# The attention products of a gated cross-attention kernel on TensorE: two 64x128 tiles in place of four 64x64 tiles

## The chip, the cores and the metric

The kernel runs on one core of one Trainium2 chip. The metric is the device time of one execution in microseconds (us), the median of several runs. A profile is one further execution, whose span (first to last instruction) is a little shorter than its time.

## The reference

Inputs in float32: `x` is 8 x 1024 x 1024, `ctx_1024` (the memory) 8 x 64 x 512, `W_mem` 1024 x 512, `W_gate` 1024 x 2048, a bias and a norm weight of 1024 each.

```python
memory_proj = jnp.einsum('bme,de->bmd', memory, W_mem)
scores = jnp.einsum('bnd,bmd->bnm', hidden_states, memory_proj) / jnp.sqrt(jnp.float32(D))
attn = jax.nn.softmax(scores, axis=-1)
memory_context = jnp.einsum('bnm,bmd->bnd', attn, memory_proj)
gate_input = jnp.concatenate([hidden_states, memory_context], axis=-1)
gate = jax.nn.sigmoid(jnp.einsum('bnf,df->bnd', gate_input, W_gate) + b_gate)
fused = hidden_states + gate * memory_context
return _rmsnorm(fused, norm_w)
```

A memory has only 64 rows, so the contraction of `attn` with anything of the memory is 64 long, half of TensorE's 128 rows.

## The kernel before

The 8192 tokens are worked in 16 query tiles (`q`) of 512 tokens, two to each of the 8 memories. The setup, up to about 80 us, computes `mp`, the projected memory, and `mg`, which is `mp` times the second half of `W_gate` plus the bias. Both are kept side by side in one tile, `mg`: partitions 0 to 63 hold `mp` of the present memory (for the context), partitions 64 to 127 hold `mp` times the gate weight (for the memory's part of the gate). `attnT` holds the softmaxed scores turned so that the 64 memory rows lie on partitions, once on 0 to 63 and once, with some sums and differences, on 64 to 127.

The large product, `x` times the first half of `W_gate`, is done for each query tile by a two-level Strassen scheme. `outer_product` (L949) handles one of seven outer products, in the order 1, 6, 7, 5, 4, 2, 3 (`ORDER`, L648); each is itself seven inner products of a 128-token block by 256 columns, issued by `product` (L961) as two 128x128 by 128x256 matmuls. The inner products go to the PSUM banks `af`, `ed` (two sets that alternate), `b` (tile `kB`) and `c` (tile `kC`). VectorE, ScalarE and GpSimd take the sums between them.

The attention enters in *visits* (`visit`, L853). A visit stands for one block of 128 tokens and one half of 512 columns, and issues two kinds of product. The first gives the context of these tokens, from partitions 0 to 63 of `attnT` and `mg` into a bank `pc`. The second adds the memory's part of the gate from partitions 64 to 127, into the bank `af` or `ed` in which the Strassen products of the same rows are summed. In one case of each four (`second and r == 0`) this second product is cut into two of 256 columns. Visits stand in blocks of four, between the inner products `kC` and `ed` of outer product 4 (visits of 5 and 4) and of outer product 3 (visits of 2 and 3). In the last query tile the second block is cut into two blocks of two visits. Before the change each product is issued twice, once for tokens 0 to 63 and once for tokens 64 to 127 (`TOKENS`, L849): as its stationary operand is 64 rows by 64 columns it takes one quarter of TensorE, and the quarter follows from the partitions of the operands and of the output. The four quarters are: upper rows or lower rows (context or gate part), left columns or right columns (first or last 64 tokens).

`scores` (L400) computes the next query tile's scores, in tiles `psT`, also in 64x64 quarters: two row halves by two column halves at each of eight steps of the depth, 32 matmuls. From the first query tile on, each `scores` of a next tile stands right behind the visits of outer product 3 in TensorE's order; the first tile's own stands alone among the inner products.

The order on each engine is the order in which the code issues (`pin`, L90); `at` and `mid` (L641, L644) put the side work at numbered slots. `mm` (L92) issues every matmul, so L93 is the line of all of them in the profile, and L96 that of all two-operand sums. A float32 matmul appears in the trace as two passes, each with its own weight load (LDWEIGHTS) and MATMUL record. In a row such as `64*64 64x512` the first pair is the rows and columns of the stationary operand, the second the moving operand.

Of the kernel before, what the change touches and what calls it, by code (L numbers as in the profile page):

```python
# [15 lines left out]
P = 128  # L16
# [4 lines left out]
def tile_gated_cross_attention_rmsnorm(  # L21
# [44 lines left out]
    M, E = mem.shape[1:]  # L66
# [25 lines left out]
    def mm(o, lhsT, rhs, start, stop):  # L92
        pin(nc.tensor.matmul(o, lhsT, rhs, start=start, stop=stop, skip_group_check=True))  # L93
# [7 lines left out]
    def t4k(pool, shape, tag, name):  # L101
        return pool.tile(shape, F32, tag=tag, name=name)
# [31 lines left out]
    for k in range(KD):  # L134
        t = t4k(*((gpool, [P, D], "gate") if k < 7 else (apool, [P, D], "s4")), f"w2_{k}")
# [363 lines left out]
    def upper(left):  # L499
        return left ^ 2 if left < 4 else left  # L500
# [345 lines left out]
    EXT = {5: (1, 1, 2), 4: (1, 0, 2), 2: (0, 0, 0), 3: (0, 1, 4)}  # L846
    SECOND = {4: 5, 3: 2}
    NEG = {4: 6, 3: 7}
    TOKENS = slice(0, P // 2), slice(P // 2, P)  # L849
    sets = 0  # L850
    held = {}

    def visit(q, o, r, pc, k, k1=None):  # L853

        row, h, g = EXT[o]
        at_, mg = attnTs[q], mgs[q // QPB]
        second = o in SECOND
        cols = slice(h * H, (h + 1) * H)
        for t in TOKENS:
            mm(pc[t, :], at_[0:M, 2 * row + r, t], mg[0:M, cols], True, True)  # L860
        if second and r == 0:
            for n, left in ((0, g + r), (1, NEG[o])):
                part = mg[M:P, h * H + n * C : h * H + (n + 1) * C]
                apart = n == 1 and k1 is not None
                for t in TOKENS:
                    dst = k1[t] if apart else k[t, n]
                    mm(dst, at_[M:P, upper(left), t], part, apart, True)
        else:
            whole = k.rearrange("p n c -> p (n c)")
            for t in TOKENS:  # L870
                mm(whole[t, :], at_[M:P, upper(g + r), t], mg[M:P, cols], second, True)

    def pre(q, o, u3, u4):

# [74 lines left out]
    def outer_product(q, o):  # L949
# [31 lines left out]
        if second:  # L981
            if alone:
                pcs = [bank(t, [P, H], f"pc{q}_{o}_{r}") for r, t in enumerate("bc")]
            else:
                f = SECOND[o]
                faf, fed, fu3, fu4 = held.pop((q, f))
                frow, fh, _ = EXT[f]
                fp = [bank(t, [P, H], f"pc{q}_{f}_{r}") for r, t in enumerate("bc")]
                pcs = [ps_ctx.tile([P, H], F32, tag="ctx", name=f"pc{q}_{o}_{r}") for r in range(2)]
                visit(q, f, 0, fp[0], faf)  # L990
                visit(q, f, 1, fp[1], fed)
            if alone:
                apart = ps_ctx.tile([P, C], F32, tag="ctx", name="apart")
                visit(q, o, 0, pcs[0], af, apart)
            else:
                visit(q, o, 0, pcs[0], af)
            visit(q, o, 1, pcs[1], ed)
# [121 lines left out]
```

## Time and profile before

| | |
|---|---|
| median of 3 runs | 945.98 us (945.97 to 946.01) |
| profiled execution: its time, its span | 945.9 us, 944.1 us |
| TensorE matmul (PE) busy | 933.0 us, 99% of the span |
| weight loads (PEld) busy, beside PE | 726.3 us, 77% |
| VectorE (DVE) busy | 798.4 us, 85% |
| GpSimd (POOL) busy | 736.7 us, 78% |
| ScalarE (ACT) busy | 420.3 us |
| MATMUL records | 5560 |

PE's busy time covers overlapping records, since several tiles work at once and a record also holds the way through the array; how much time a stage takes is read from the starts of the records. A query tile takes 53.35 us in the steady part (the visits' first block starts at 217.37, 270.72 and 324.07 us).

### The profile page before, as it was taken

What the parts mean: (1) busy time and instruction counts of PE and PEld (TensorE: products, weight loads), DVE (VectorE), ACT (ScalarE), POOL (GpSimd) and SP (SyncE); (2) the same over time, 40 slices, a digit from 0 to 9 for tenths busy, and PEclk for the clock granted to TensorE, in tenths of its full rate; (3) what the DMA queues carried; (4) which work ended last, traced back from release to release, by engine and by line L of the source; (5) the groups of instructions that cost most, each with busy time, mean ns of one, the idle gap of its engine ahead of it and who ended that gap; (6) DMA issues with size and microseconds to landing.
All of it is one profiled execution on the core that took longest, in us unless ns stands there. A gap on an engine that the chain in (4) does not pass through costs nothing.

```text
span 944.1 us, 15840 instructions
## 1 busy us (share of the span) xinstructions
PE 933.0 (99%) x5560; PEld 726.3 (77%) x5560; DVE 798.4 (85%) x1273; ACT 420.3 (45%) x1089; POOL 736.7 (78%) x815
## 2 busy tenths in 40 slices
PE   9999999999999999999999999999999999999995
PEld 8546778787877778787877778687877778787774
DVE  6989888888887888888887888888887888888887
ACT  3001437263644527263643627263543617264556
POOL 5998968788586868778596868778696868868695
PEclk9999999999999999999999999999999999999998
DMA  9956664482919365491919366391918456391632
GB/s 377 287 149 157 112 124 111 113 179 48 209 45 182 99 137 131 103 187 41 216 46 175 93 143 137 90 201 32 220 51 168 102 134 146 80 205 33 134 153 90
DMA packets 70928, 128.44 MB, mean 136 GB/s; under 512 B 12352, under 2 KB 49216, under 8 KB 70592
## 3 DMA queue, kind: packets, MB, share of 16 engines
q1 hardware_dynamic: 61664, 93.86, 37.8%
q0 software_dynamic: 9184, 33.56, 19.5%
q8 instruction: 45, 0.74, 0.3%
q14 instruction: 35, 0.29, 0.1%
HBM read 87.56 MB, written 41.68 MB: 137 GB/s over the span
## 4 chain that ended last, share of the span: by engine, by line
PE 94%; DVE 3%; POOL 1%; issue 1%; ACT 1%; POOLq 0%; DVEq 0%; ACTq 0%
PE af L93 31%; PE ed L93 20%; PE pc L93 10%; PE kC L93 10%; PE kB L93 10%; PE pg L93 5%; PE psT_af L93 5%; PE pm L93 3%; POOL gate L96 1%; DVE gate L96 1%; DVE u L96 0%; PE psT_ed L93 0%; PE pz L93 0%; PE psT_b L93 0%; POOL l L96 0%
## 5 line engine op out<-in xcount | busy, mean ns | idle before, releaser
L96 POOL TENSOR_TENSOR gate<-gate,u 128x512 f32<-128x512 f32 (+1 forms) x224 | 243.5, 1099 | 153.7 <-DVE u L96 152.8
L717 ACT ACTIVATE gate<-gate 128x512 f32<-128x512 f32 x127 | 79.9, 630 | 181.5 <-DVE gate L96 180.0
L353 DVE STREAM_TRANSPOSE a<-xq 128x512 f32<-128x512 f32 x128 | 141.6, 1110 | 11.0 <-PE af L93 7.7
L96 POOL TENSOR_TENSOR l<-a 128x256 f32<-128x256 f32 x128 | 110.0, 859 | 17.1 <-PE af L93 15.9
L93 PE MATMUL pc<-mg,attnT 64*64 64x512 f32 x512 | 117.0, 596 | 0.3 <-DVE u L96 0.3
L971 ACT COPY u<-af 128x256 f32<-128x256 f32 x112 | 41.4, 370 | 166.0 <-PE af L93 151.2
L93 PE MATMUL kB<-it,l 128*128 128x256 f32 x448 | 115.0, 379 | 0.0
L93 PE MATMUL ed<-it,l 128*128 128x256 f32 x448 | 115.0, 379 | 0.0
L746 DVE SCALAR_TENSOR_TENSOR gate<-gate,ss,nw_sb 128x512 f32<-128x512 f32 x120 | 109.7, 914 | 1.1
L93 PE MATMUL af<-w,a 128*128 128x256 f32 x384 | 98.5, 379 | 0.0
L96 DVE TENSOR_TENSOR gate<-gate,pc 128x512 f32<-128x512 f32 x128 | 85.5, 677 | 11.8 <-ACT gate L717 11.8
L93 PEld LDWEIGHTS kB<-it,l 128*128 128x128 f32 x448 | 85.1, 190 | 11.6
L93 PEld LDWEIGHTS ed<-it,l 128*128 128x128 f32 x448 | 85.1, 190 | 11.6
L96 DVE TENSOR_TENSOR gate<-gate,ed 128x512 f32<-128x512 f32 x112 | 76.3, 682 | 16.2 <-POOL gate L96 14.1
L96 DVE TENSOR_TENSOR gate<-gate,af 128x512 f32<-128x512 f32 (+1 forms) x128 | 76.0, 604 | 13.1 <-PE af L93 10.4
L96 POOL TENSOR_TENSOR l<-s 128x256 f32<-128x256 f32 x96 | 84.0, 875 | 3.0 <-PE af L93 3.0
L93 PEld LDWEIGHTS af<-w,a 128*128 128x128 f32 x384 | 73.0, 190 | 10.3 <-issue 0.5
L96 DVE TENSOR_TENSOR u<-u,kB 128x256 f32<-128x256 f32 x112 | 45.9, 409 | 33.2 <-PE kB L93 31.4
L93 PEld LDWEIGHTS pc<-mg,attnT 64*64 64x64 f32 x512 | 32.8, 132 | 49.9 <-issue 23.2
L93 PE MATMUL ed<-it,a 128*128 128x256 f32 x256 | 67.4, 386 | 0.0
L93 PE MATMUL af<-mg,attnT 64*64 64x512 f32 (+1 forms) x380 | 67.0, 457 | 0.0
L93 PE MATMUL af<-t,s 128*128 128x256 f32 x256 | 65.8, 380 | 0.0
(155 smaller groups left out, 2113.4 us busy)
## 6 DMA issues: line engine op xcount, KB each, us to landing
xq<-in_x SPq DMA_DIRECT2D x64, 512.0 KB, 10.1
gate<-in_x POOLq DMA_DIRECT2D x60, 512.0 KB, 8.1
out<-gate SPq DMA_DIRECT2D x60, 512.0 KB, 2.9
w<-in_w_gate_t SPq DMA_DIRECT2D x8, 512.0 KB, 10.2
w<-in_w_gate_t SPq DMA_DIRECT2D x2, 2048.0 KB, 16.7
mg<-mgd SPq DMA_DIRECT2D x16, 256.0 KB, 4.8
wm<-in_w_mem_t SPq DMA_DIRECT2D x4, 512.0 KB, 6.1
mpd<-mpT SPq DMA_DIRECT2D x4, 512.0 KB, 8.5
```

The costliest lines, as they stand in the source:

```text
L93: pin(nc.tensor.matmul(o, lhsT, rhs, start=start, stop=stop, skip_group_check=True))
L96: pin(eng.tensor_tensor(o, a, b, op))
L353: nc.vector.transpose(A[key][:, :, r * P : (r + 1) * P], chunks(xq[q][:, 4 * t : 4 * t + 4, :], KD)[:, half * KH : (half + 1) * KH],)
L717: pin(nc.scalar.activation(g, g, AF.Sigmoid))
L746: nc.vector.scalar_tensor_tensor(g[:, cols], g[:, cols], rstd[:, t % 2 : t % 2 + 1], nw_sb[:, cols], ALU.mult, ALU.mult,)
L971: pin(nc.scalar.copy(p1, af[:, 0]))
```

## The change

`visit` issues each of its products once for all 128 tokens. The stationary operand is now 64 rows by 128 columns and takes one row half of TensorE: the context product the upper 64 rows, the gate part the lower 64, beside each other. Nothing else is edited; `scores` keeps its 64x64 quarters.

```diff
-    TOKENS = slice(0, P // 2), slice(P // 2, P)
...
-        for t in TOKENS:
-            mm(pc[t, :], at_[0:M, 2 * row + r, t], mg[0:M, cols], True, True)
+        mm(pc, at_[0:M, 2 * row + r, :], mg[0:M, cols], True, True)
         if second and r == 0:
             for n, left in ((0, g + r), (1, NEG[o])):
                 part = mg[M:P, h * H + n * C : h * H + (n + 1) * C]
                 apart = n == 1 and k1 is not None
-                for t in TOKENS:
-                    dst = k1[t] if apart else k[t, n]
-                    mm(dst, at_[M:P, upper(left), t], part, apart, True)
+                mm(k1 if apart else k[:, n], at_[M:P, upper(left), :], part, apart, True)
         else:
-            whole = k.rearrange("p n c -> p (n c)")
-            for t in TOKENS:
-                mm(whole[t, :], at_[M:P, upper(g + r), t], mg[M:P, cols], second, True)
+            mm(k.rearrange("p n c -> p (n c)"), at_[M:P, upper(g + r), :], mg[M:P, cols], second, True)
```

On TensorE, at the block of visits in outer product 4 of the first query tile, this stands before (the last pair of numbers is the output's size; `pc`, `af` and `ed` are the banks named above, and the numbers behind them name the outer product and the buffer):

```order
L93 MATMUL kC_4_734<-t_420,l_0_4_686 128x256 x2
L93 MATMUL pc_5_0_739<-mg_482,attnT_666 64x512 x2
L93 MATMUL af_5_679<-mg_482,attnT_666 64x512 x2
L93 MATMUL pc_5_1_740<-mg_482,attnT_666 64x512 x2
L93 MATMUL ed_5_680<-mg_482,attnT_666 64x512 x2
L93 MATMUL pc_4_0_741<-mg_482,attnT_666 64x512 x2
L93 MATMUL af_4_719<-mg_482,attnT_666 64x256 x4
L93 MATMUL pc_4_1_742<-mg_482,attnT_666 64x512 x2
L93 MATMUL ed_4_720<-mg_482,attnT_666 64x512 x2
L93 MATMUL ed_4_720<-it_421,a_0_462 128x256 x2
```

With the change it is this:

```order
L93 MATMUL kC_4_734<-t_420,l_0_4_686 128x256 x2
L93 MATMUL pc_5_0_739<-mg_482,attnT_666 128x512
L93 MATMUL af_5_679<-mg_482,attnT_666 128x512
L93 MATMUL pc_5_1_740<-mg_482,attnT_666 128x512
L93 MATMUL ed_5_680<-mg_482,attnT_666 128x512
L93 MATMUL pc_4_0_741<-mg_482,attnT_666 128x512
L93 MATMUL af_4_719<-mg_482,attnT_666 128x256 x2
L93 MATMUL pc_4_1_742<-mg_482,attnT_666 128x512
L93 MATMUL ed_4_720<-mg_482,attnT_666 128x512
L93 MATMUL ed_4_720<-it_421,a_0_462 128x256 x2
```

Nothing has moved: each pair of half-token products is one product at the same place, between the inner products `kC` and `ed`.

On TensorE, at the end of the visits in outer product 3 of the first query tile, where the scores of the second one begin, this stands before:

```order
L93 MATMUL pc_3_1_846<-mg_482,attnT_666 64x512 x2
L93 MATMUL ed_3_822<-mg_482,attnT_666 64x512 x2
L93 MATMUL psT_af_870<-a_1_672,mpb_358 64x256
L93 MATMUL psT_af_870<-a_1_699,mpb_358 64x256
L93 MATMUL psT_ed_871<-a_1_672,mpb_358 64x256
```

And this with the change:

```order
L93 MATMUL pc_3_1_837<-mg_482,attnT_666 128x512
L93 MATMUL ed_3_813<-mg_482,attnT_666 128x512
L93 MATMUL psT_af_852<-a_1_672,mpb_358 64x256
L93 MATMUL psT_af_852<-a_1_699,mpb_358 64x256
L93 MATMUL psT_ed_853<-a_1_672,mpb_358 64x256
```

Before, the visits and the scores behind them are of one shape, 64x64; now the shape changes between them. The orders of VectorE, ScalarE, GpSimd and the DMA queues differ only in the numbers of buffers.

## The prediction

> **What bounds the kernel now.** I read the page first: engines, clock, and the chain that ended last.
>
> ```profile
> span 944.1 us, 15840 instructions
> PE 933.0 (99%) x5560; PEld 726.3 (77%) x5560; DVE 798.4 (85%) x1273; ACT 420.3 (45%) x1089; POOL 736.7 (78%) x815
> PEclk9999999999999999999999999999999999999998
> PE 94%; DVE 3%; POOL 1%; issue 1%; ACT 1%; POOLq 0%; DVEq 0%; ACTq 0%
> ```
>
> PE carries 94% of the chain at full clock. Whether others hold it up is in the view of the waits, for PE alone, and in the view of windows over one query tile (span, then each engine's busy time).
>
> ```profile
> PE pz L93 <- DVE zeros L116: 1.2, 1, 1.2
> PE pc L93 <- DVE u L96: 0.3, 1, 0.3
> 217.30:270.70 53.40, 53.40 (x333) 42.43 (x332) 45.29 (x75) 25.46 (x67) 41.40 (x49) 1.00 0.55 124
> ```
>
> PE waits twice in the whole run, 1.5 us together, and in this query tile it has no idle time. So what the change adds to PE's stretch of a block, or takes from it, reaches the end one to one; no other engine can hide it. But a busy PE is not yet a streaming PE, and for this change the starts of records count. The timeline of PE around one block of visits (start, length, names, shapes):
>
> ```profile
> 216.41 1.03 PE L93 MATMUL kC<-t,l 128*128 128x256 f32 x4
> 217.37 0.65 PE L93 MATMUL pc<-mg,attnT 64*64 64x512 f32 x2
> 217.38 0.65 PE L93 MATMUL af<-mg,attnT 64*64 64x512 f32 x2
> 217.85 0.60 PE L93 MATMUL pc<-mg,attnT 64*64 64x512 f32 x2
> 217.86 0.60 PE L93 MATMUL af<-mg,attnT 64*64 64x512 f32 x2
> 218.28 0.60 PE L93 MATMUL pc<-mg,attnT 64*64 64x512 f32 x2
> 218.29 0.60 PE L93 MATMUL ed<-mg,attnT 64*64 64x512 f32 x2
> ...
> 220.42 0.60 PE L93 MATMUL pc<-mg,attnT 64*64 64x512 f32 x2
> 220.44 0.60 PE L93 MATMUL ed<-mg,attnT 64*64 64x512 f32 x2
> 220.97 1.13 PE L93 MATMUL ed<-it,a 128*128 128x256 f32 x4
> 221.93 1.03 PE L93 MATMUL ed<-it,l 128*128 128x256 f32 x4
> 222.80 1.03 PE L93 MATMUL af<-t,l 128*128 128x256 f32 x4
> ```
>
> Three things are in it. First, the four quarters stream together: the first pass of both token halves of `pc` and of `af` starts within 0.02 us, the second passes 0.43 us after that in the steady part, so a visit takes two steps of 0.43, 0.86 us. Second, the inner products follow each other every 0.87 us (221.93 to 222.80), but `pc` starts 0.96 after `kC`: a gap of 0.09 to 0.10 on the way in. On the way out the last passes start at 220.42 and 220.44, stream 0.43 and end at 220.87; the next product starts at 220.97, again 0.10 later. Third, the first pass behind each gap is longer, 0.65 for 0.60 and 1.13 for 1.03: its weights were not loaded ahead. Single records say by how much, in the view by tile (minimum, median and maximum in ns):
>
> ```profile
> L93 PE MATMUL pc<-mg,attnT x512: 588/589/641, 110.7 to 930.2; 64*64 64x512 f32 x171
> L93 PE MATMUL ed<-it,a x256: 378/379/483, 82.3 to 921.3; 128*128 128x256 f32 x128
> ```
>
> A first load of 64 columns costs 641 - 589 = 52 ns, one of 128 columns 483 - 379 = 104 ns. Where the shape stays, at the end of the visits in front of the scores, the timeline shows none of this:
>
> ```profile
> 236.30 0.60 PE L93 MATMUL pc<-mg,attnT 64*64 64x512 f32 x2
> 236.32 0.59 PE L93 MATMUL ed<-mg,attnT 64*64 64x512 f32 x2
> 236.73 0.38 PE L93 MATMUL psT_af<-a,mpb 64*64 64x256 f32 x2
> 236.75 0.38 PE L93 MATMUL psT_ed<-a,mpb 64*64 64x256 f32 x2
> ...
> 239.97 0.38 PE L93 MATMUL psT_af<-a,mpb 64*64 64x256 f32 x2
> 239.99 0.38 PE L93 MATMUL psT_ed<-a,mpb 64*64 64x256 f32 x2
> 240.30 1.13 PE L93 MATMUL ed<-it,s 128*128 128x256 f32 x4
> ```
>
> The scores start 0.43 after the last visit's pass, as if they were a further visit, with a first pass of ordinary length; the gap and the long first pass come behind the scores, where the shape changes (239.99 plus a pass of 0.21 is 240.20).
>
> **The change part by part.** How often: the `pc` row counts 512 passes; a visit has two passes for each of two token halves, so there are 128 visits, in 32 blocks of which the last is cut in two: 33 blocks. The first way in that doesn't wait for VectorE and the last one show that the gap is the same throughout:
>
> ```profile
> 125.59 1.03 PE L93 MATMUL kC<-w,l 128*128 128x256 f32 x4
> 126.55 0.65 PE L93 MATMUL pc<-mg,attnT 64*64 64x512 f32 x2
> ...
> 927.92 1.03 PE L93 MATMUL kC<-w,l 128*128 128x256 f32 x4
> 928.87 0.65 PE L93 MATMUL pc<-mg,attnT 64*64 64x512 f32 x2
> L93 PE MATMUL psT_af<-a,mpb x480: 375/376/377, 130.0 to 880.2; 64*64 64x256 f32 x160
> ```
>
> Both are 0.95 to 0.96. Scores behind visits: 480 passes of `psT_af`, 32 to one query tile, so 15 times.
>
> *Streaming.* Four quarters with two passes each become two halves with two passes each, a pass still 0.43: 0.86 us a visit as before, as long as the two halves run together. Price nothing. The cover of the loads: a 128-column load has 0.43 of streaming over it, and in the split product of 256 columns still 0.21. The nearest row for that is the inner products, where loads of 190 ns under passes of this length leave no gap:
>
> ```profile
> L93 PEld LDWEIGHTS kB<-it,l 128*128 128x128 f32 x448 | 85.1, 190 | 11.6
> 217.95 0.14 PEld L93 LDWEIGHTS pc<-mg,attnT 64*64 64x64 f32 x2 [0.38 <-DVE u L96]
> ```
>
> The second row (timeline of the weight loads) is the one load that something else delays: the second visit's `pc` takes the bank of `kC` and waits for VectorE until 217.95, then loads until 218.09, 0.19 ahead of its pass at 218.28. A load of 0.19 ends at 218.14, still 0.14 ahead, and 0.05 more if the block's first load takes that much longer. If this cover were gone, the other visits' products would queue behind it on PE.
>
> *First load of a block.* 128 columns instead of 64. I take the difference of the two rows above, 104 - 52 = 0.052 us, 33 times: +1.7 us. Bounds: nothing, if a half's load works on two column quarters at once (52 ns as now); and 0.156 us, 33 times or 5.1, if the two row halves load one behind the other. I take the middle since the two row halves load together now (the first passes of `pc` and `af` start within 0.02).
>
> *Block's end.* Of the four quarters the last start 0.02 behind the first (220.42, 220.44), and the way out waits for them. With two halves about half of this goes: -0.01, 33 times, -0.3 us. Bounds -0.7 and 0.
>
> *Visits to scores.* This shape change is new, 15 times, and no row shows a change from 64x128 to 64x64. The nearest are the changes between 128x128 and 64x64: a gap of 0.10, a first load of 52 ns, and the 0.01 by which the scores no longer start tile by tile while the last half ends; 0.16, 15 times, +2.4 us. Bounds: nothing (or a hundredth less than nothing each, the shorter stagger), if halves and quarters count as one shape since the row split is the same; 0.22 or 3.3, if it costs like a way out, gap and 104 ns. I take 0.16 because in all places seen a changed shape brings the gap, and only an unchanged one (236.73) lacks it. The Trainium skill says the same of it: in TensorEngine Tiling (Array Packing), Key Properties, a change of the tiling mode, not of the tile alone, drains TensorE, and its list has 64x128 and 64x64 as different modes. By that rule the term is what I take; this is the rule that speaks against the change.
>
> *The way in and out otherwise.* 128x128 to 64x128 instead of to 64x64, and back: I leave the gaps of 0.10 as they are. *Other engines.* Half the matmul instructions in the visits are gone, but PE never waited for its instructions there. The sums behind `pc` wait for the same product at the same place.
>
> Sum: +1.7 - 0.3 + 2.4 = +3.8 us on the profiled 945.9, 949.7. The median of the runs, 945.98, lies 0.08 above: 949.8 us, 0.4% slower. A difference of 0.2%, 1.9 us, is about what a measurement of this kernel can tell from no change.
>
> **The rivals.**
>
> *A: as summed*, 949.8.
>
> *B: 64x128 and 64x64 are one shape for the switch.* For it: both split the rows alike, and every gap in the trace stands where both rows and columns changed, so the trace can't tell which counts. Against it: no changed shape in the trace goes without a gap. The term of 2.4 goes: 947.4, within 0.2%. If instead the switch costs and the first load stays at 52 ns, it is +2.1, 948.1, just outside.
>
> *C: the way into and out of halves is cheap; faster.* If it is the split into columns that makes the gap, a block of halves follows a 128x128 product like any product, its weights loaded ahead. Then 33 ways in save 0.10 + 0.05, 4.9 us; the 18 ways out that lead to inner products save 0.10 + 0.10, 3.6 us; the 15 ways into the scores still cost 2.4. That is -6.1, 939.9. It decides from the point where a way in is cheaper by 0.07 of its 0.15: then 33 of them pay the 15 new ones. For it: all gaps seen lead to or from column-split tiles. Against it: the rows are split in them too, and a half must be loaded while a full-array product streams over the same rows.
>
> *D: loads of the two halves one after the other.* 0.104 more at each of 33 blocks: 949.8 + 3.4 = 953.2. For it: both halves use the whole width of the array. Against: 64-column loads in both row halves go together now.
>
> *E: the halves don't overlap as assumed.* The order on PE is `pc`, then `af`, and each is two passes. If passes start strictly in that order, `af`'s first pass goes with `pc`'s second, and each block is one pass longer: 33 x 0.43 = 14, 964. If the halves don't overlap at all, because the lowering doesn't split the rows and the change is not what it says, each of 128 visits takes two steps more: 128 x 0.86 = 110, 1056. Against both: `af` starts at 217.38 with `pc`'s first pass, ahead of `pc`'s second at 217.85. The Trainium skill, in TensorE: Matmul & The Clock Gate, Part 3, says that matmuls start and end in strict program order. By that rule the first of these would come out; the trace of before disagrees with it for quarters, by those two starts.
>
> **How the numbers follow.** A 0.52, B 0.21 (0.15 for 947.4, 0.06 for 948.1), C 0.13, D 0.10, E 0.04 (half for each of its times). The time is A's, 949.8. The range leaves out C and E, 17 in 100: low 946.9, which is B's 947.4 with the lower bounds of the stagger, 0.4 and 15 x 0.01; high 953.6, D's 953.2 with half of the 0.9 that the switch costs more at its upper bound. Slower by over 0.2% (above 947.9): A, D, E and B's second case, 0.72. Within 0.2%: B's first, 0.15. Faster: C, 0.13.
>
> **What would show it.** In the changed profile: `pc` as 64*128 with half the records, passes 0.43 apart with `af` or `ed` 0.01 behind; block entries with a first pass of about 693 for 589 ns; a gap of 0.10 and a long first pass at the scores; a query tile of 53.35 + (2 x 0.04 + 0.16) = 53.6 us. Passes of `pc` and `af` in turn would mean E. No gap at a block's entry would mean C, none at the scores B. A new wait of PE for VectorE at the second visit would mean that I misjudged the cover there.

## The result, and the profile after

The changed kernel takes 950.10 us (median of 5 runs, 949.81 to 950.19), the kernel before 945.98; the ratio is 1.0041 with a 95% interval of 1.003 to 1.0052. The forecast was 949.8 and slower. The profiled execution has a span of 948.3 us, 4.2 more than before.

The page shows what left the kernel and that the bound has not moved:

```profile
span 948.3 us, 14687 instructions
PE 937.1 (99%) x4984; PEld 737.0 (78%) x4984; DVE 799.8 (84%) x1273; ACT 420.3 (44%) x1089; POOL 736.4 (78%) x815
PE 95%; DVE 2%; issue 1%; POOL 1%; DMA 1%; ACT 1%; SPq 0%; POOLq 0%; DVEq 0%; ACTq 0%
```

TensorE has 576 matmuls and as many loads fewer, and is 4.1 us busier. Its waits are the same two as before:

```profile
PE pz L93 <- DVE zeros L116: 1.2, 1, 1.2
PE pc L93 <- DVE u L96: 0.5, 1, 0.5
```

The timeline of PE around the block of visits that the prediction read (start, length, names, shapes):

```profile
217.48 1.03 PE L93 MATMUL kC<-t,l 128*128 128x256 f32 x4
218.43 0.69 PE L93 MATMUL pc<-mg,attnT 64*128 64x512 f32 x1
218.44 0.69 PE L93 MATMUL af<-mg,attnT 64*128 64x512 f32 x1
218.97 0.59 PE L93 MATMUL pc<-mg,attnT 64*128 64x512 f32 x1
218.97 0.59 PE L93 MATMUL af<-mg,attnT 64*128 64x512 f32 x1
219.40 0.59 PE L93 MATMUL pc<-mg,attnT 64*128 64x512 f32 x1
219.40 0.59 PE L93 MATMUL ed<-mg,attnT 64*128 64x512 f32 x1
...
221.54 0.59 PE L93 MATMUL pc<-mg,attnT 64*128 64x512 f32 x1
221.55 0.59 PE L93 MATMUL ed<-mg,attnT 64*128 64x512 f32 x1
222.07 1.13 PE L93 MATMUL ed<-it,a 128*128 128x256 f32 x4
...
272.02 0.69 PE L93 MATMUL pc<-mg,attnT 64*128 64x512 f32 x1
```

The two halves start within 0.01 us of each other and step by 0.43, as the four quarters did. `pc` still starts 0.95 after `kC`, so the gap on the way in is the old one; the first pass is 0.69 long instead of 0.65, and the second comes 0.53 to 0.54 after it instead of 0.48. The way out is the old one as well: the next product starts 0.52 after the last `ed` pass, where before it was 0.53 (220.44 to 220.97). From the first pass of the block to the product behind it, it is 3.64 instead of 3.60. The last row is the same block one query tile later: a query tile takes 272.02 - 218.43 = 53.59 us instead of 53.35, 0.24 more, which leaves 0.16 beside the 0.04 of each of its two blocks.

At the end of the second block the scores no longer follow as if they were a visit:

```profile
237.47 0.59 PE L93 MATMUL pc<-mg,attnT 64*128 64x512 f32 x1
237.48 0.59 PE L93 MATMUL ed<-mg,attnT 64*128 64x512 f32 x1
238.00 0.43 PE L93 MATMUL psT_af<-a,mpb 64*64 64x256 f32 x2
238.01 0.43 PE L93 MATMUL psT_ed<-a,mpb 64*64 64x256 f32 x2
238.26 0.38 PE L93 MATMUL psT_af<-a,mpb 64*64 64x256 f32 x2
```

They start 0.53 after the last `pc` pass instead of 0.43, and the next round 0.26 later instead of 0.22. The view by tile has the single records (minimum, median and maximum in ns, then the first and last start in us):

```profile
L93 PE MATMUL pc<-mg,attnT x256: 589/589/693, 111.3 to 934.5; 64*128 64x512 f32 x128
L93 PE MATMUL psT_af<-a,mpb x480: 376/376/427, 130.8 to 884.4; 64*64 64x256 f32 x160
```

The first load of a block costs 693 - 589 = 104 ns, and that of the scores 427 - 376 = 51 ns where it cost nothing. The stretch from the first `pc` to the last was 930.2 - 110.7 = 819.5 us and is 934.5 - 111.3 = 823.2 us: 3.7 more. Another 0.6 lies ahead of the first visit (111.3 for 110.7), where the change edits nothing. In the experiments below the first visit starts between 110.9 and 112.6, without order by the number of changed blocks: 111.5 in the kernel in which half of the blocks changed, 110.9 in its complement. What moves it is not shown, so some 0.4 of the 4.1 us in the medians is not accounted for by the change of shape.

### The profile page after: what moved, and what is told of

Its sections match the earlier page's. It is cut to its first block, busy times and chain, and to the rows that moved or that the text cites. A ratio compares the mean times of both kernels' runs of the same rounds, so it can differ in the third digit from the quotient of the medians.

```text
span 948.3 us, 14687 instructions
## 1 busy us (share of the span) xinstructions
PE 937.1 (99%) x4984; PEld 737.0 (78%) x4984; DVE 799.8 (84%) x1273; ACT 420.3 (44%) x1089; POOL 736.4 (78%) x815
## 4 chain that ended last, share of the span: by engine, by line
PE 95%; DVE 2%; issue 1%; POOL 1%; DMA 1%; ACT 1%; SPq 0%; POOLq 0%; DVEq 0%; ACTq 0%
PE af L93 31%; PE ed L93 20%; PE pc L93 11%; PE kB L93 10%; PE kC L93 10%; PE psT_af L93 5%; PE pg L93 5%; PE pm L93 2%; DMA wm<-in_w_mem_t 1%; POOL gate L96 1%; DVE u L96 0%; PE psT_b L93 0%; PE psT_ed L93 0%; DVE gate L96 0%; DVE mx L459 0%
## 5 line engine op out<-in xcount | busy, mean ns | idle before, releaser
L96 POOL TENSOR_TENSOR l<-a 128x256 f32<-128x256 f32 x128 | 112.1, 876 | 17.0 <-PE af L93 15.8
L93 PE MATMUL pc<-mg,attnT 64*128 64x512 f32 x256 | 118.6, 602 | 0.5 <-DVE u L96 0.5
L96 DVE TENSOR_TENSOR gate<-gate,pc 128x512 f32<-128x512 f32 x128 | 85.5, 677 | 11.8 <-ACT gate L717 11.8
L93 PEld LDWEIGHTS pc<-mg,attnT 64*128 64x128 f32 x256 | 45.1, 186 | 42.4 <-issue 21.2
L93 PE MATMUL af<-mg,attnT 64*128 64x512 f32 (+1 forms) x190 | 68.3, 466 | 0.0
```

What stands on the lines that cost most here:

```text
L96: pin(eng.tensor_tensor(o, a, b, op))
```

## The experiments

Theory S is that of the prediction: a change of the tile's shape on TensorE costs a gap of 0.09 to 0.10 us and a first load that grows with its columns, nothing else in the change costs anything, and all of it lands because TensorE never waits. The first rival, H, spreads the loss over the time in which halves run. The others belong to single runs. The kernel before, run again beside each group of experiments, had medians of 945.95 to 946.09 us. The edits of the scores (in halves, and one product later) are made to the changed kernel, all others to the kernel before.

### Halves between 128x128 products only, and halves ahead of the scores only

In the first kernel the condition is `o in (5, 4)`, in the second its complement, `o in (2, 3)`:

```diff
-    TOKENS = slice(0, P // 2), slice(P // 2, P)
+    HALVES = slice(0, P // 2), slice(P // 2, P)
+    WHOLE = (slice(0, P),)
...
+        TOKENS = WHOLE if o in (5, 4) else HALVES
```

> Halves (64x128) only in the 16 blocks of visits in outer product 4, which lie between two 128x128 products; the other blocks keep quarters (64x64). Theory S (only changes of the tile's shape cost): 16 x 0.042 us for the wider first load less the shorter stagger, +0.7 us over the kernel before, 946.7; a steady query tile of 53.39 us instead of 53.35. Theory H (halves cost while they run, the 4.1 us of the whole change spread evenly over its 33 blocks, 0.125 each): 16 x 0.125 = +2.0, 948.0; a query tile of 53.47.

> The complement: halves only in the 17 blocks behind outer products 2 and 3, 15 of which the scores in quarters follow. Theory S: 17 x 0.042 + 15 x 0.16 = +3.1 us over the kernel before, 949.1; a steady query tile of 53.55 us. Theory H: 17 x 0.125 = +2.1, 948.1, a query tile of 53.47.

Measured: 946.89 us (ratio 1.0005, interval 0.9996 to 1.0014) and 949.18 (1.0026, 1.0016 to 1.0036). S said 946.7 and 949.1, H 948.0 and 948.1. The block alone, in the first kernel, from one query tile to the next:

```profile
163.97 1.03 PE L93 MATMUL kC<-t,l 128*128 128x256 f32 x4
164.93 0.69 PE L93 MATMUL pc<-mg,attnT 64*128 64x512 f32 x1
...
217.36 1.03 PE L93 MATMUL kC<-t,l 128*128 128x256 f32 x4
218.32 0.69 PE L93 MATMUL pc<-mg,attnT 64*128 64x512 f32 x1
```

The query tile takes 218.32 - 164.93 = 53.39 us, 0.04 more than before; S had 53.39, H 53.47. In the second kernel it takes 53.55 us (from 164.48 to 218.03), where S had 53.55 and H 53.47. The time of the first kernel alone can't be told from that of the kernel before, as its interval holds 1; but H's 948.0, a ratio of 1.002, lies outside it. About as many blocks cost 0.9 us between products and 3.2 ahead of scores in quarters. H falls.

### The scores in halves too

```diff
-                for r in range(2):
-                    mm(
-                        pst[g][r * M : (r + 1) * M, :],
-                        mpb[rows, k, :],
-                        A[q, r, k // KH][rows, k % KH, :],
-                        k == 0,
-                        k == KD - 1,
-                    )
+                pair = mpb[rows, k // 2 * 2 : k // 2 * 2 + 2, :].rearrange("p a m -> p (a m)")
+                mm(pst[g], pair, A[q, k % 2, k // KH][rows, k % KH, :], k == 0, k == KD - 1)
```

> Visits in halves as in the changed kernel, and the scores in halves too: the stationary operand is two neighbouring depth steps of the memory, 128 columns, and each round streams one of the two token blocks only, so the passes keep their number of steps but half of the scores' products are left out and the scores are not the reference's. Theory S: no change of shape between visits and scores, so the 2.4 us of the changed kernel that belong to it go: 945.98 + 34 x 0.042 = 947.4, and a steady query tile of 53.43 us. If the scores start late behind halves whatever their own shape: 949.8.

Measured: 947.55 us (1.0019, 1.001 to 1.0028), where S had 947.4; a query tile takes 53.43 us (165.79 to 219.22), as S had it. With the same shape on both sides the scores start 0.43 behind the last visit again, their first pass of ordinary length:

```profile
184.82 0.59 PE L93 MATMUL pc<-mg,attnT 64*128 64x512 f32 x1
184.83 0.59 PE L93 MATMUL ed<-mg,attnT 64*128 64x512 f32 x1
185.25 0.38 PE L93 MATMUL psT_af<-a,mpb 64*128 64x256 f32 x1
185.26 0.38 PE L93 MATMUL psT_ed<-a,mpb 64*128 64x256 f32 x1
```

So the scores do not start late behind halves as such; it is the difference of the shapes.

### The scores one product later

```diff
-        mid((q, 3), scores, q + 1)
-        at(t0 + 46, add_scores, q + 1)
+        at(t0 + 46, scores, q + 1)
+        at(t0 + 47, add_scores, q + 1)
```

> All visits in halves as in the changed kernel, but the scores moved behind the next 128x128 product, so that they no longer follow the visits. Theory S: in place of one change from halves to quarters (gap 0.09 and first load 0.05) there is one out to the product (0.09 and 0.10) and one in to the scores (0.10 and 0.05): +0.20, 15 times, 3.0 us over the changed kernel, 953.1. Theory P (the scores start late behind the visits because of a bank or an operand that they wait for, not because of the shape): one product later the wait is over, -0.14, 15 times, 2.2 us under the changed kernel, 947.9.

Measured: 953.23 us (1.0074, 1.0059 to 1.009); S had 953.1, P 947.9. A query tile takes 53.79 us (164.81 to 218.60), 0.20 more than in the changed kernel, as S had it. The product now between them pays for its own way in, and the scores for theirs:

```profile
183.84 0.59 PE L93 MATMUL pc<-mg,attnT 64*128 64x512 f32 x1
183.86 0.59 PE L93 MATMUL ed<-mg,attnT 64*128 64x512 f32 x1
184.38 1.13 PE L93 MATMUL ed<-it,s 128*128 128x256 f32 x4
185.44 0.43 PE L93 MATMUL psT_af<-a,mpb 64*64 64x256 f32 x2
```

Theory P falls: one product later the scores cost more and not less, and their first pass is 0.43 long here too.

### Halves and quarters by turns

The condition above is `r == 0`: in each block the visits alternate.

> In every block the visits take turns: halves, quarters, halves, quarters; the last one has the shape of the scores. Theory S: per block of four visits 0.05 for the wider first load, 0.16 for each of two changes from halves to quarters and 0.21 (gap 0.09, first load 0.10, stagger 0.02) for the change from quarters to halves, which no run has shown so far: 0.58, 31 times, and 0.21 for the two blocks of two visits: +18.4 us over the kernel before, 964.4. If the change from quarters to halves is free, 957.9. Theory H (0.031 for each visit in halves): half of the visits, +2.1, 948.1.

Measured: 963.71 us (1.018, 1.0166 to 1.0194), 17.7 more than before, where S had 18.4 and H 2.1; S is 0.02 too high for each block. This kernel has the one change that no run had shown, from quarters to halves:

```profile
165.88 0.59 PE L93 MATMUL pc<-mg,attnT 64*128 64x512 f32 x1
165.88 0.59 PE L93 MATMUL af<-mg,attnT 64*128 64x512 f32 x1
166.40 0.65 PE L93 MATMUL pc<-mg,attnT 64*64 64x512 f32 x2
166.42 0.65 PE L93 MATMUL ed<-mg,attnT 64*64 64x512 f32 x2
166.88 0.59 PE L93 MATMUL pc<-mg,attnT 64*64 64x512 f32 x2
166.90 0.60 PE L93 MATMUL ed<-mg,attnT 64*64 64x512 f32 x2
167.42 0.69 PE L93 MATMUL pc<-mg,attnT 64*128 64x512 f32 x1
```

Each change, in either direction, puts 0.52 to 0.54 between the starts of `pc` in place of 0.43, and the first pass behind it is long by its columns, 0.65 or 0.69.

### Both shapes inside one visit

```diff
-        for t in TOKENS:
-            mm(pc[t, :], at_[0:M, 2 * row + r, t], mg[0:M, cols], True, True)
+        mm(pc, at_[0:M, 2 * row + r, :], mg[0:M, cols], True, True)
```

> Inside each visit the context product in one half (64x128) and the gate part in two quarters (64x64). Theory S: two shapes never stream together, so a visit takes four steps of 0.43 us instead of two and changes shape twice, 0.14 and 0.22: 128 x 1.22 - 33 x 0.22 + 33 x 0.05 = +151 us, 1097. Theory I (the row halves are independent, each with its own split into columns): the two run together, within 4 us of the kernel before, under 950.

Measured: 1095.46 us, in a single run; S had 1097. Although the two products use different row halves, they take turns, each with two steps of 0.43, a first load and a gap:

```profile
195.27 1.12 PE L93 MATMUL pc<-mg,attnT 64*128 64x512 f32 x2
196.32 1.08 PE L93 MATMUL af<-mg,attnT 64*64 64x512 f32 x4
197.32 1.12 PE L93 MATMUL pc<-mg,attnT 64*128 64x512 f32 x2
```

A visit takes 2.05 us instead of 0.86: halves and quarters did not overlap. Theory I falls.

### Eighths: a miss, and what it was

```diff
-    TOKENS = slice(0, P // 2), slice(P // 2, P)
+    TOKENS = [slice(i * 32, (i + 1) * 32) for i in range(4)]
```

> The visits in 64x32 tiles, eight at once, the scores in quarters as before. Theory S: the first load of a block has 32 columns, 0.026 us for 0.052, -0.9 in 33 blocks; eight tiles start over about 0.05 instead of 0.02, +1.0; visits and scores differ again in shape, 15 x 0.17 = +2.6: 948.7. If only the way from halves to quarters costs, because the array is split further there, and not the way back: 946.1.

> Visits and scores both in 64x32 tiles. Theory S: one shape again, so the 15 changes cost nothing; the narrower first load, 34 x -0.026 = -0.9, against the longer stagger of eight tiles at each way out, 34 x 0.03 = +1.0: 946.1, the same as the kernel before. If eight tiles stagger no more than four do: 945.1, the fastest of all. If twice the instructions can't be issued in the scores' steps of 0.22 us: over 947.

Measured: 956.42 us (1.0106, 1.0092 to 1.0119) and 957.91 (1.0121, 1.0105 to 1.0136): 7.7 and 11.8 above S, so neither is a way to a faster kernel. The load by columns is as expected; in the first of the two, by tile:

```profile
L93 PE MATMUL pc<-mg,attnT x1024: 588/589/614, 111.5 to 939.6; 64*32 64x512 f32 x171
```

32 columns cost 614 - 589 = 25 ns. The loss stands in the last visit of a block:

```profile
168.00 0.61 PE L93 MATMUL pc<-mg,attnT 64*32 64x512 f32 x4
168.03 0.81 PE L93 MATMUL ed<-mg,attnT 64*32 64x512 f32 x4
168.43 0.61 PE L93 MATMUL pc<-mg,attnT 64*32 64x512 f32 x4
168.46 0.81 PE L93 MATMUL ed<-mg,attnT 64*32 64x512 f32 x4
```

A group of four `ed` tiles is 0.81 long where others are 0.61: three of the four start about 0.2 late. Twice in a query tile this is 0.40, and with the 0.16 of the scores the tile takes 53.91 us instead of 53.35. A wait that holds the group as a whole, as in theory V below, does not fit: the group's first tile was loaded 0.22 us ahead of its pass, while the other loads of the group come only from 168.03 on, as the weight loads show:

```profile
167.81 0.11 PEld L93 LDWEIGHTS ed<-mg,attnT 64*32 64x32 f32 x1
168.00 0.13 PEld L93 LDWEIGHTS pc<-mg,attnT 64*32 64x32 f32 x4
168.03 0.33 PEld L93 LDWEIGHTS ed<-mg,attnT 64*32 64x32 f32 x7
```

That led to one more kernel, which issues the same products and moves only the context product of one visit in each block:

```diff
-        for t in TOKENS:
+        split = second and r == 0
+        for t in () if split else TOKENS:
             mm(pc[t, :], at_[0:M, 2 * row + r, t], mg[0:M, cols], True, True)
...
                 for t in TOKENS:
                     dst = k1[t] if apart else k[t, n]
                     mm(dst, at_[M:P, upper(left), t], part, apart, True)
+                for t in TOKENS if n == 0 else ():
+                    mm(pc[t, :], at_[0:M, 2 * row + r, t], mg[0:M, cols], True, True)
```

> The visits in 64x32 tiles again, with one difference in order: in the visit whose gate product is cut into two of 256 columns, the context product stands between the two and not ahead of both. In the earlier 64x32 kernel the last visit's gate tiles start 0.16 to 0.19 us late. Theory W (TensorE looks ahead over 64 records of loads and matmuls): there the late load stands 65 records behind the oldest pass that was still on its way (13 left of the context product, 32 of the cut one, 16 of the next context product, 4 of the gate tile ahead); woven it is about 49, the lateness goes, and with it 0.20 in 32 blocks, 6.4 us: 950.0, a steady query tile of 53.51 us instead of 53.91. Theory V (the gate product waits for its own semaphore, which this order keeps): 956.4, 53.91.

Measured: 949.89 us (1.0036, 1.0023 to 1.0048); W had 950.0, V 956.4. The same four rows:

```profile
167.49 0.61 PE L93 MATMUL pc<-mg,attnT 64*32 64x512 f32 x4
167.52 0.61 PE L93 MATMUL ed<-mg,attnT 64*32 64x512 f32 x4
167.92 0.61 PE L93 MATMUL pc<-mg,attnT 64*32 64x512 f32 x4
167.95 0.61 PE L93 MATMUL ed<-mg,attnT 64*32 64x512 f32 x4
```

The lateness is gone and the query tile takes 53.51 us, as W had it. What is shown is that the order decides and that the semaphore, which both kernels wait for, does not (V falls). Where the limit lies is only counted: in the late group the first tile's load stands 61 records behind the oldest pass by W's count (13 + 32 + 16) and was on time, the second one's 65 and was late. The Trainium skill, in TensorE: Matmul & The Clock Gate, Part 3, states a reorder window 64 deep, and this agrees. In the kernel with eighths in the scores too, the two late visits are the same 0.40; in seven query tiles the scores run late besides, by 0.2 to 1.0 us. PE waits there for the issue of instructions four times, 1.3 us in all; why it does, and what makes the rest of the delay, is open.

## Why the prediction was right

- *All of it lands on TensorE.* Right. PE's two waits stayed, and in the kernels with halves a query tile moved by what the starts of its blocks and scores show.
- *Streaming costs nothing.* Right: steps of 0.43 before and after. Rival E needed `pc` and `af` to take turns; they start 0.01 apart.
- *First load of a block,* 0.052, 33 times. Right: 104 against 52 ns. Rival D needed the second half's load to wait for the first; both first passes are 0.69 long. The second time of rival E, 1056, was added to the kernel before and not to the forecast as the first was; it should read 1060, and nothing rests on it.
- *Block's end,* -0.01, 33 times. Right: the block is 0.04 longer and the load alone is 0.05.
- *Visits to scores,* +2.4, a change of shape that no row of before showed. Right: 0.16 in a query tile, 15 times. By the rows, which are rounded to the hundredth, the scores start 0.10 later, gap and lost overlap together, and their first load of 51 ns comes on top. In the kernels where the scores follow quarters, follow halves as halves, or follow a product, it went and came as S had it. Rival B, that only the split of rows counts for the shape, falls here; so does C, for which only the split of columns would. From 128x128 to 64x128 only the rows change, from 64x128 to 64x64 only the columns, and both bring the gap of 0.09 to 0.10.
- *The sum.* +3.8 forecast; 3.7 between the first and the last visit, 4.1 in the medians. The mechanism accounts for the 3.7; the rest arose ahead of the first visit, which the forecast did not consider, and that it was small is luck. The rule that the prediction took from the Trainium skill (TensorEngine Tiling (Array Packing), Key Properties: a change of mode drains) agrees with every change that these kernels make, each of which left its gap.

## What to carry to other kernels

Choose TensorE's tile shape by its neighbours in the order, not by how few instructions it takes: two halves stream as much as four quarters, and the shape that the next product shares is the cheaper one. To price a change of shape on a busy TensorE, count the places where the shape changes and read one of them from the starts of the records: here 0.10 us of gap and the first load, 0.05 us for 64 columns. Products of 64x128 and 64x64 did not overlap at all here, although they use different rows of the array, so a mixed pair cost whole passes and not a tenth of a microsecond; other pairs of shapes were not tried side by side.

## What the runs showed of the hardware

- The first load behind a change of shape showed 25, 52 and 104 ns for 32, 64 and 128 columns. For 128 columns it was the same for one tile (128x128) and for two beside each other (64x128).
- Matmuls of different tiles start out of the order in which the kernel issues them: in the kernel before, the gate product's first pass starts 0.47 us ahead of the context product's second, which stands ahead of it.
- That freedom ends: with the late load 65 records behind the oldest pass on its way the tiles came about 0.2 us late, with 61 and with about 49 they were on time. With half as many tiles, as in the kernel before, the same count is about 33, and its visits show no such lateness.
